# Half products for each tile of nodes in a graph layer, with the first group of rows tile by tile and the end of the last stage reordered

## The chip, the cores and the metric

The kernel runs on one core of a Trainium2 chip. A core has five engines, each with an instruction queue that it works off in order: TensorE (PE, matrix products; its weight loads are listed as PEld), VectorE (DVE), ScalarE (ACT), GpSimd (POOL) and SyncE (SP, which only issues transfers). Transfers are carried out by DMA engines and are issued by SP, ACT and POOL. The metric is the time of one execution on the device in microseconds (us). All times in the tables below are from one profiled execution, unless the text says that they are the medians of timed runs.

## The reference

The layer takes 6250 nodes with 256 features, and 100000 edges sorted by target, with 64 features each.

```python
xn = layernorm(x)
x1 = x + gnn(xn) + mix(xn)
out = x1 + ffn(layernorm(x1))

# gnn: messages along edges, summed by target
msg  = relu(xn[src] + edge_attr @ We + be)
z    = xn + segment_sum(msg, dst, N)
h    = relu(relu(z @ W1 + b1) @ W2 + b2) + xn
gnn  = layernorm(h) * gamma + beta

# mix: linear attention with 8 heads, then an MLP 256 -> 1024 -> 256
xm  = layernorm(xn) * ln1_w + ln1_b ;  xm = xm @ Wx.T + bx
q, k, v = softmax(xm Wq, features), softmax(xm Wk, nodes), xm Wv
h   = q @ (k.T @ v) @ Wo.T + bo + xn
mix = gelu(layernorm2(h) @ W1.T + b1) @ W2.T + b2 + h

# ffn: 4 experts; the gates come from a 4-head graph attention over the same edges
#   (with self loops): softmax over each node's incoming edges, layernorm, top 2 of 4
ffn = sum over experts e of  gate[:, e] * (gelu(x W1[e] + b1[e]) @ W2[e] + b2[e])
```

All of it is computed in float32.

## The kernel before

**Tiles.** Nodes lie in 49 tiles of 128 rows (the last is shorter), in 13 groups of up to four tiles. Edges lie in blocks: a block (q, 99 of them) has eight tiles of 128 edge slots and serves a window of 128 nodes. Windows advance by 64 nodes from block to block, so a tile of nodes k gets its sums from the blocks around 2k, and a block of even q serves the upper half of one node tile and the lower half of the next.

**Phase A** (to about 98 us) loads x group by group, normalises it twice (the layer's own norm, then that of the mixer), stores the rows xb that the edges will gather and the rows z that the sums are added to, and makes xm, stored as xmT. For each group DVE takes the statistics, ACT the square roots (L258), DVE the reciprocals and shifts (L262, L263), ACT the affine y (L266), DVE xn (L547), POOL xb (L550). It also reads edge indices and checks that they fit the blocks; a branch at its end (L434) takes another way for edges that don't.

**Phase B** (about 98 to 1276 us) has two strands that share the engines.

- The edge strand. POOL gathers rows of xb by the edges' sources, 128 rows in a transfer, 782 transfers (L408), into four buffers of four tiles each. TensorE multiplies the edge features by We into PSUM (msg, L1241), DVE adds the gathered rows (m, L1227, frees the gather's buffer), ACT applies the relu (L1229). For each block DVE builds two selection matrices: S, that says which slot of 32 an edge adds to (L1212), and W, that says which node of the window a slot belongs to (L1215). TensorE multiplies S with m into ps (L1259; four groups of columns, 32 wide), ACT copies ps to SBUF (left, L1263), TensorE multiplies W with left (win, L1266), DVE adds win to the rows of z (add_sums, L1188).
- The node strand. First the key-value part of the attention over all nodes, with a sort of the edges' keys (L677, L678 on DVE, L687 on TensorE); then for each group of nodes attention (attn, L1000), the mixer's MLP (L1040, L1056), and, when the sums of the group are in, the graph's MLP (L1082, L1093, z at L1104) and the norm of the result, with the head products of the graph attention (hT, L1166).

**Phase C** (about 1278 to 2407 us) runs the four experts on TensorE (L1611, L1629, outputs to DRAM as y) while POOL gathers a 32-wide row for each edge in sorted order, 784 transfers (G, L1329), in 14 chunks. DVE turns each chunk into running softmax sums by scans along the edges (attend, L1409 to L1455; the sums are stored to DRAM as sum_d, L1458). When a range of nodes has its sums, POOL gathers them (gm, L1653), share computes the gates, and weigh loads a tile's y and x1 (L1753, L1755), weighs the four experts on DVE (L1759), and stores the output (L1762). The tail after the last G gather has the last two chunks, the last gates and the last six tiles of outputs.

**What sets the order.** Each strand is a Python generator whose steps name an engine, a guessed length, what buffers they take and drop, and a rank. A planner (`Plan`) goes through all steps with the guessed lengths: it takes the step that can begin first, and among those on that engine that can begin nearly as early, the one of the lowest rank. The order that results is written out by hand as each engine's queue: the guesses decide the order, the chip decides the times. A gather of four tiles is guessed at 5.0 us and one of phase C at 1.255 us.

The number of PSUM banks for general use in phase B is four, beside two double buffers for msg.

In phase B the code around the window product, before, is:

```python
            yield step(PE, mm(1, 256), take=["bank"], drop=["left", "W"], rank=of_edges)
            pw = bank("win")
            nc.tensor.matmul(pw[:, :D], W[p0:p1, :], left[p0:p1, :], start=True, stop=True)
```

Of the kernel before, what the change touches and what calls it, by code (L numbers as in the profile page):

```python
# [17 lines left out]
P = 128  # L18
# [118 lines left out]
def gps_layer_kernel(ctx: ExitStack, tc: tile.TileContext, a: dict, out: bass.AP):  # L137
# [7 lines left out]
    NUE = a["srcT"].shape[1]  # L145
    assert NUE % 2 == 0 and NU - EG < NUE <= NU
    CG = NE // P
# [63 lines left out]

    def load_row(name, n, pool=const, col0=0):

        t = pool.tile([P, n], F32, name="r_" + name)
        src = a[name]
        nc.scalar.dma_start(t, bass.AP(tensor=src.tensor, offset=src.offset, ap=[[0, P], [1, n]]))
        return t
# [106 lines left out]

    load_x(0)
    load_x(1)
    be = load_row("be", D, ep)
    wx = load("WxT", [P, KD, D], ep)
    ln1w = load("ln1_w", [P, KD], ep)
    ln1b = load("ln1_b", [P, KD], ep)  # L330
    bx = load("bx", [P, KD], ep)
    bdq = eb.tile([P, P], F32, name="bdq")
# [159 lines left out]
    for g in range(NG + 3):  # L492
        if g < NG:
            t0, nt, cols = group(g)
            xt = xts.pop(g)
            load_x(g + XAHEAD)
            for i in range(nt):
                ln_stats(mu_var[:, t0 + i, :], xt[:, i, :], rows(t0 + i), pa)
            rs2 = pa.tile([P, GW], F32, tag="rs2", name="rs2")
            nm2 = pa.tile([P, GW], F32, tag="nm2", name="nm2")  # L500
            for r, f, n in parts(t0, nt):
                ts = slice(t0 + f, t0 + f + n)
                ln_root(rs1[:, ts], mu_var[:, ts, :], r)

                ln_root(rs2[:, f:f + n], mu_var[:, ts, :], r, scale=1.0 + EPS, add=eps2)
# [31 lines left out]
        if g < NG:  # L537
            t0, nt, cols = group(g)
            xn = pa.tile([P, GW, D], F32, tag="xn", name="xn")
            xb = pa.tile([P, GW, D], F32, tag="xb", name="xb")  # L540
            y = ys[g] = pa.tile([P, GW, D], F32, tag="y", name="y")
            for r, f, n in parts(t0, nt):
                ts = slice(t0 + f, t0 + f + n)
                ln_shift(rs1[:, ts], nm1[:, ts], mu_var[:, ts, :], r)
                ln_shift(rs2[:, f:f + n], nm2[:, f:f + n], mu_var[:, ts, :], r)
                for i in range(f, f + n):
                    nc.vector.tensor_scalar(xn[:r, i, :], xt[:r, i, :], mu_var[:r, t0 + i, 0:1],  # L547
                                            rs1[:r, t0 + i:t0 + i + 1], op0=OP.subtract, op1=OP.mult)
                    affine(y[:, i, :], xt[:, i, :], r, rs2[:, i:i + 1], nm2[:, i:i + 1])
                nc.gpsimd.tensor_tensor(xb[:r, f:f + n, :], xn[:r, f:f + n, :],  # L550
                                        be[:r].unsqueeze(1).to_broadcast([r, n, D]), OP.add)
                nc.sync.dma_start(node_rows(xb_d, t0, r, f, n), xb[:r, f:f + n, :])
                nc.sync.dma_start(node_rows(z0_d, t0, r, f, n), xn[:r, f:f + n, :])
# [21 lines left out]
    nc.vector.tensor_copy(kmr, pr[:, :KD * P].rearrange("p (k c) -> p k c", k=KD))  # L575
    by_hand.close()
    early.close()
# [3 lines left out]
    pmsg = psum.enter_context(tc.tile_pool(name="pmsg", bufs=2, space=PSUM))  # L581
    by_hand = ctx.enter_context(ExitStack())
    by_hand.enter_context(tc.manual_schedule(engines=EVERY))

# [79 lines left out]
    def sort():  # L664
# [72 lines left out]
        for w in sorted({w for _, w in chunks}, reverse=True):  # L737
            first = [o for o, w_ in chunks if w_ == w]
            o0 = first[0]
            for o in first:  # L740
                if o == first[-1] or o + w * P not in first:
# [13 lines left out]
    plan = Plan(dict(bank=4, msg=2, xm=0, x=NXH, x_=1, hm=NXH, hm_=1, r4=R4, hT=1, qT=2, xn=1, mv=6,  # L755
                     xg=XG - 0, ea=EA, S=2, W=2, m=2, left=2, z=ZB))
    plan.when.update({("xm", 0, g): 0.0 for g in first_order[:2]})
# [422 lines left out]

    def add_sums(pw, k, p0, p1):

        if not 0 <= k < NT:
            return
        p1 = min(p1, rows(k))
        if p0 < p1:
            z = zs[k // GW]
            nc.vector.tensor_add(z[p0:p1, k % GW, :], z[p0:p1, k % GW, :], pw[p0:p1, :D])  # L1188

    def sum_loads():  # L1190
# [16 lines left out]
    def block_kinds():  # L1207

        for q in range(NQ):
# [3 lines left out]
                                    slot[:, q * EG:(q + 1) * EG].unsqueeze(2).to_broadcast([P, EG, SLOT]), OP.is_equal)  # L1213
            W = ew.tile([P, P], F32, tag="W", name="W", bufs=2)
            nc.vector.tensor_scalar(W, iotaf if q % 2 else iotah, spot[:, q:q + 1], None, op0=OP.is_equal)  # L1215
# [28 lines left out]
    def sums():  # L1244

        for q in range(NQ):
            hs = halves(q)
# [8 lines left out]
            for b in range(2):  # L1256
                for i in tiles[b::2]:
                    j = i // 2
                    nc.tensor.matmul(ps[j * SLOT:(j + 1) * SLOT, :D], S[:, i, :], ms[i // 4][:, i % 4, :],  # L1259
                                     start=b == 0, stop=b == 1)  # L1260
            yield step(ACT, act(256), take=["left"], drop=["bank"], rank=0)
            left = ew.tile([P, D], F32, tag="left", name="left", bufs=2)
            nc.scalar.activation(left[p0:p1], ps[p0:p1, :D], AF.Copy)  # L1263
            yield step(PE, mm(1, 256), take=["bank"], drop=["left", "W"], rank=of_edges)
            pw = bank("win")
            nc.tensor.matmul(pw[:, :D], W[p0:p1, :], left[p0:p1, :], start=True, stop=True)  # L1266
            yield step(DVE, vec(256, 1 if q % 2 else 2), drop=["bank"], rank=1, give=[("sums", q)],
                       need=[("z", min(k // GW, NG - 1)) for k in ([q // 2] if q % 2 else [max(q // 2 - 1, 0), q // 2])])
            if q % 2:
                add_sums(pw, q // 2, 0, P)  # L1270
            else:
                add_sums(pw, q // 2 - 1, P // 2, P)
                add_sums(pw, q // 2, 0, P // 2)

# [42 lines left out]
    assert len(sure) == early[-1][2]  # L1317
    GBUFS, RING, PREP = 5, 7, 4
    SLOTS = dict(bank=6, at=2, G=GBUFS, A=2, prep=PREP, ring=RING, yo=3, hT=2, lT=2, ac=4)
    plan = Plan(SLOTS)  # L1320
# [69 lines left out]
    def attend(o, w):  # L1390

        R = 0 if w < CW else 2
        yield step(DVE, vec(4 * w, 2) + vec(0), rank=R, take=["at"], need=[("ready", o), ("G", o)])
# [12 lines left out]

        yield step(DVE, 0.35 * NH + vec(0, 2), rank=R)
        for h in range(NH):
# [5 lines left out]
        cm = yield from carried(T2, D2, NH, OP.add, OP.max, car[1], "car1", o)  # L1414
        yield step(DVE, 0.35 * NH + vec(0), rank=R)
        M = tl("M", NH, w + 1)
# [25 lines left out]
        for c0 in range(0, ROW, 5):  # L1442
            yield step(DVE, 0.3 * 5, rank=R)
            for c in range(c0, c0 + 5):
                nc.vector.tensor_tensor_scan(S[:, c, :], dk[:, head[c], :], G[:, :, c], 0.0, op0=OP.mult, op1=OP.add)
# [6 lines left out]
        for c0 in range(0, ROW, 5):  # L1452
            yield step(DVE, 0.35 * 5, rank=R, drop=["at", "prep"] * (c0 + 5 == ROW))
            for c in range(c0, c0 + 5):
# [188 lines left out]
    def share(t0, t1, need):  # L1643

        R = 4 if t1 < NT else 0
        ts, n = slice(t0, t1), t1 - t0
# [101 lines left out]
    def weigh(t, need, gates):  # L1748

        r, b = rows(t), t * P  # L1750
        yield step(SP, 0.8, rank=4, take=["ring", "ac"], need=need)
        y = ring([NX, D], F32, "y")
        nc.sync.dma_start(y[:r], y_d[t // GW, :r, :, t % GW, :])  # L1753
        ac = pc.tile([P, D], F32, tag="ac", name="ac", bufs=4)
        nc.sync.dma_start(ac[:r, :], x1_d[b:b + r, :])  # L1755
        for e in range(0, NX, 2):
            yield step(DVE, 1.0, rank=5 if t < early[-1][0] else 0, drop=["ring"] * (e == NX - 2), need=gates)
            for e_ in range(e, e + 2):
                nc.vector.scalar_tensor_tensor(ac[:r, :], y[:r, e_, :], gate[:r, t, e_:e_ + 1], ac[:r, :],  # L1759
                                               op0=OP.mult, op1=OP.add)  # L1760
        yield step(SP, 0.4, rank=4, drop=["ac"])
        nc.sync.dma_start(out[b:b + r, :], ac[:r, :])  # L1762

    def shares(some):
        for t0, t1, c in some:
            if t1 == NT:

                yield step(SP, 0, need=[("gate", early[-3][0])])
                for t in range(t0, t1):
                    spawn(weigh(t, [("y", t // GW, e) for e in range(NX)], [("gate", t0)]))  # L1770
                yield from share(t0, t1, [("sum", chunks[c - 1][0])])
                return
            yield from share(t0, t1, [("sum", chunks[c - 1][0])])
            for t in range(t0, t1):
                spawn(weigh(t, [("y", t // GW, e) for e in range(NX)], [("gate", t0)]))

    spawn = plan.spawn
    for thread in (gathers_of(sure), places(), experts(), scatter_starts(), prepare(sure), shares(early[:-1]), shares(early[-1:])):
        spawn(thread)
# [105 lines left out]
```

## Time and profile before

| what | us |
|---|---|
| timed runs, median of 3 (lowest to highest) | 2468.9 (2466.7 to 2469.7) |
| the profiled execution, its own time | 2467.7 |
| its span | 2465.9 |
| PE busy | 1997.3 |
| DVE busy | 1590.8 |
| ACT busy | 898.9 |
| POOL busy | 1703.3 |
| 782 gathers of edge rows (L408), busy | 795.1 |
| 784 gathers of phase C (L1329), busy | 768.5 |
| first gather of phase C starts | 1278.5 |
| last gather of phase C starts | 2406.4 |

A group's row in the profile gives the line, the engine, the operation, output and input by the program's names with their shapes, how many of them there were, then their busy time together and the mean of one in ns, and at the end the engine's idle time just before them and what it was that ended most of it. A row of the timeline gives the start in us, the length, the same names, how many records it stands for, and in brackets the idle time before it. A TensorE product in float32 is two records. Matrix products are pipelined, so the sum of their records may exceed the time that they take. A row of waits gives the waiting engine and operation, what it waited for, the total, the number of times and the longest. Times of the execution are shown against the span's start.

### The profile page before, as it was taken

The page shows a single profiled execution, that of the slowest core. Times are in us where ns is not written, and L with a number is a line of the kernel's source. Part 1 is how long each engine was busy: PE and PEld are TensorE (multiplying, and loading weights), DVE is VectorE, ACT ScalarE, POOL GpSimd, SP SyncE. Part 2 cuts the span into 40 slices and gives each one's busy share as a digit, 9 for nine tenths or more (in the row PEclk, how much of TensorE's full clock was granted, in tenths as well). Part 3 has the DMA queues.
Part 4 walks back from the last instruction along what each step waited for, and adds up shares of the span by engine and source line. Part 5 has one row for each costly group of instructions (what it writes and reads, how often), then busy time and mean ns, then how long its engine had stood idle before and what let it go on. Part 6 is the DMA issues. An engine that isn't in the chain of part 4 may idle for free.

```text
span 2465.9 us, 30623 instructions
## 1 busy us (share of the span) xinstructions
PE 1997.3 (81%) x10156; PEld 1297.9 (53%) x10156; DVE 1590.8 (65%) x4328; ACT 898.9 (36%) x1429; POOL 1703.3 (69%) x1701
## 2 busy tenths in 40 slices
PE   6897889998899898999969999978578898986000
PEld 3484555565565565566546776644245565655000
DVE  7588886674687786888736771119757456426566
ACT  5544645555555455665521002112222131212001
POOL 5417777777677777777327777777777777777771
PEclk9998999999999998999989999989789999998555
DMA  8865457767655545554341111212335445224522
GB/s 261 283 198 177 141 156 226 225 192 241 205 148 152 159 132 166 155 149 122 93 133 25 13 46 52 62 45 78 85 95 181 113 137 167 67 57 113 176 50 72
DMA packets 243957, 329.65 MB, mean 134 GB/s; under 512 B 49504, under 2 KB 187010, under 8 KB 242374
## 3 DMA queue, kind: packets, MB, share of 16 engines
q1 hardware_dynamic: 176678, 209.82, 26.1%
q0 software_dynamic: 65776, 116.46, 19.1%
q8 instruction: 84, 1.38, 0.2%
q10 hardware_dynamic: 1328, 1.26, 0.2%
q14 instruction: 91, 0.75, 0.1%
HBM read 227.34 MB, written 100.04 MB: 133 GB/s over the span
## 4 chain that ended last, share of the span: by engine, by line
POOL 35%; PE 25%; issue 14%; DVE 10%; DMA 9%; ACT 2%; SPq 0%; DVEq 0%; POOLq 0%; ACTq 0%
POOL G L1329 22%; POOL xg L408 9%; DMA xg<-xb_d,srcI 6%; PE hist L1491 5%; PE ffn L1040 3%; DVE m L1227 3%; PE msg L1241 3%; PE ffn L1056 3%; PE e L1629 2%; POOL st_d L1563 2%; POOL gm L1653 2%; PE e L1611 2%; PE g L1093 1%; PE ps L1259 1%; PE g L1082 1%
## 5 line engine op out<-in xcount | busy, mean ns | idle before, releaser
L408 POOL DMA_INDIRECT xg<-xb_d,srcI x782 | 795.1, 1017 | 314.3 <-issue 208.1
L1329 POOL DMA_INDIRECT G<-tab_d,srcs x784 | 768.5, 980 | 317.5 <-issue 238.6
L1589 ACT ACTIVATE hT<-e,w_eb 128x512 f32<-128x512 f32 (+1 forms) x208 | 136.3, 661 | 732.8 <-PE e L1629 712.0
L1629 PE MATMUL e<-lT,ew 128*128 128x512 f32 (+1 forms) x832 | 365.9, 587 | 17.6 <-DMA lT<-xlT_d 10.4
L1611 PE MATMUL e<-ew,hT 128*128 128x256 f32 (+1 forms) x1568 | 364.4, 389 | 4.0 <-DVE yo L1593 1.6
L1611 PEld LDWEIGHTS e<-ew,hT 128*128 128x128 f32 (+1 forms) x1568 | 302.5, 195 | 68.8 <-issue 21.1
L1227 DVE TENSOR_TENSOR m<-msg,xg 128x1024 f32<-128x1024 f32 x196 | 234.1, 1217 | 128.3 <-DMA xg<-xb_d,srcI 78.0
L1229 ACT ACTIVATE m<-m 128x1024 f32<-128x1024 f32 x196 | 205.7, 1053 | 187.9 <-DVE m L1227 184.4
L1241 PE MATMUL msg<-we,ea 64*128 64x256 f32 x1564 | 225.6, 415 | 48.7 <-DVE m L1227 43.6
L1629 PEld LDWEIGHTS e<-lT,ew 128*128 128x128 f32 x832 | 153.7, 195 | 178.8 <-issue 152.6
L1593 DVE TENSOR_TENSOR yo<-e,b 128x256 f32<-128x256 f32 (+1 forms) x196 | 79.0, 419 | 233.2 <-PE e L1611 233.1
L1241 PEld LDWEIGHTS msg<-we,ea 64*128 64x128 f32 x1564 | 143.5, 194 | 130.3 <-DVE m L1227 88.7
L1341 PE MATMUL cT<-ident,T 128*4 128x128 f32 (+1 forms) x42 | 13.4, 319 | 223.1 <-DVE T L1411 70.4
L1040 PE MATMUL ffn<-yT,w_mW1T 128*128 128x512 f32 (+1 forms) x416 | 191.3, 587 | 1.0 <-ACT hT L1030 0.5
L1056 PE MATMUL ffn<-w_mW2T,hT 128*128 128x256 f32 (+1 forms) x784 | 187.5, 387 | 0.0
L1056 PEld LDWEIGHTS ffn<-w_mW2T,hT 128*128 128x128 f32 (+1 forms) x784 | 146.0, 191 | 36.9 <-issue 15.2
L1501 DVE TENSOR_TENSOR oh<-iotar,hl 128x1024 bf16<-128x1024 bf16 (+1 forms) x256 | 123.1, 555 | 43.4 <-PE hist L1491 43.4
L1491 PE MATMUL hist<-oh 128*64 128x128 bf16 x1024 | 125.7, 418 | 9.5 <-DMA b<-in_eb 9.5
L1341 PEld LDWEIGHTS cT<-ident,T 128*4 128x4 f32 (+1 forms) x42 | 3.6, 86 | 232.1 <-issue 121.0
L1259 PE MATMUL ps<-m,S 128*32 128x256 f32 x1564 | 110.0, 397 | 15.4 <-ACT yT L1018 7.7
L1491 PEld LDWEIGHTS <-oh 128*64 128x64 bf16 x1024 | 101.6, 198 | 37.0 <-issue 12.6
L1040 PEld LDWEIGHTS ffn<-yT,w_mW1T 128*128 128x128 f32 x416 | 74.7, 195 | 73.6 <-issue 67.2
(382 smaller groups left out, 2909.9 us busy)
## 6 DMA issues: line engine op xcount, KB each, us to landing
ea<-in_eaQ SPq DMA_DIRECT2D x99, 256.0 KB
y_d<-yo SPq DMA_DIRECT2D x48, 512.0 KB
y<-y_d SPq DMA_DIRECT2D x48, 512.0 KB
sum_d<-zf SPq DMA_DIRECT2D x32, 512.0 KB
G<-tab_d,srcs POOLq DMA_INDIRECT x784
xg<-xb_d,srcI POOLq DMA_INDIRECT x782
xm<-xmT_d SPq DMA_DIRECT2D x23, 512.0 KB
sum_d<-G SPq DMA_DIRECT2D x11, 1024.0 KB
```

Of the source, the lines that this page charges most:

```text
L408: nc.gpsimd.indirect_dma_start(out=xg, out_offset=None, in_=xb_d[:, :], in_offset=bass.IndirectOffsetOnAxis(ap=srcI[:, u:u + 1], axis=0))
L1040: nc.tensor.matmul(ps[:, :cols], mw1[:, k, c * P:(c + 1) * P], yTs[g][:, k, :cols], start=k == 0, stop=k == KD - 1)
L1056: nc.tensor.matmul(ps[:r, :D], hT[0][:, c, i * P:i * P + r], mw2[:, c, :], start=c == 0, stop=c == MC - 1)
L1227: nc.vector.tensor_add(m[:, :n, :], ps[:, :n, :], xgs.pop(q * EG + 4 * s)[:, :n, :])
L1229: nc.scalar.activation(m[:, :n, :], m[:, :n, :], AF.Relu)
L1241: nc.tensor.matmul(ps[:, i % 4, :], lh, rh, start=True, stop=True)
L1259: nc.tensor.matmul(ps[j * SLOT:(j + 1) * SLOT, :D], S[:, i, :], ms[i // 4][:, i % 4, :], start=b == 0, stop=b == 1)
L1329: nc.gpsimd.indirect_dma_start(out=rows_of[o][:, c, :], out_offset=None, in_=tab_d[:, :], in_offset=bass.IndirectOffsetOnAxis(ap=srcs[:, o ...
L1491: nc.tensor.matmul(hist[0][b * KHI:(b + 1) * KHI, :P], hi[:, :, b * HG // 2 + i], lo[:, :, b * HG // 2 + i], start=c0 + i == 0, stop=c0 + ...
L1589: nc.scalar.activation(hT[:, c, :cols], ps[:, :cols], AF.Gelu, bias=b1[:, e * XC + c:e * XC + c + 1])
L1611: nc.tensor.matmul(ps[:r, :D], hT[:, c, i * P:i * P + r], w2s[e][:, c, :], start=c == 0, stop=c == XC - 1)
L1629: nc.tensor.matmul(ps[:, :cols], w1s[e][:, k, c * P:(c + 1) * P], lTs[g][:, k, :cols], start=k == 0, stop=k == KD - 1)
```

## The change

- Group 0 of x is loaded as four transfers, one for each tile, and all work of phase A on it that took the group at once (roots, shifts, affine, xn, xb, the stores) goes by tiles. The loads of be, WxT, ln1_w, ln1_b and bx are issued by SP, not by ACT.
- The hand-written order is no longer closed and opened again between phase A and phase B.
- In phase B the window product of a block (128 columns) becomes half products: for each tile of nodes, once the three blocks that touch it have their `left`, four products of 64 columns each accumulate into one PSUM bank, and DVE adds the bank to the tile's rows of z once. W has five buffers for two, left four for two; a `left` that isn't filled over all 128 rows is cleared first.
- In phase C there are eight buffers for ac, not four; the last chunk's `attend` goes ahead of the others in rank; the scans' guessed lengths depend on the chunk's width; `share` and `weigh` have other ranks; the loads for the last two ranges of nodes (tiles 43 to 48) are made known to the planner once the gates of tiles 39 to 42 are done, and those tiles' outputs are stored by ACT, not by SP.

```diff
-    load_x(0)
+    def pieces(g, t0, nt):
+        return [(P, i, 1) for i in range(nt)] if g == 0 else parts(t0, nt)
+    xts[0] = pa.tile([P, GW, D], F32, tag="xt", name="xt", bufs=XAHEAD + 2)
+    for r, f, n in pieces(0, 0, GW):
+        nc.sync.dma_start(xts[0][:r, f:f + n, :], node_rows(a["x"], 0, r, f, n))
     load_x(1)
-    be = load_row("be", D, ep)
-    wx = load("WxT", [P, KD, D], ep)
+    be = load_row("be", D, ep, nc.sync)
+    wx = load("WxT", [P, KD, D], ep, nc.sync)
...
-            for i in range(nt):
-                ln_stats(mu_var[:, t0 + i, :], xt[:, i, :], rows(t0 + i), pa)
-            for r, f, n in parts(t0, nt):
+            for r, f, n in pieces(g, t0, nt):
                 ts = slice(t0 + f, t0 + f + n)
+                for i in range(f, f + n):
+                    ln_stats(mu_var[:, t0 + i, :], xt[:, i, :], r, pa)
...
-    by_hand.close()
     early.close()
     psum.close()
...
-    by_hand = ctx.enter_context(ExitStack())
-    by_hand.enter_context(tc.manual_schedule(engines=EVERY))
...
-                     xg=XG - 0, ea=EA, S=2, W=2, m=2, left=2, z=ZB))
+                     xg=XG - 0, ea=EA, S=2, W=5, m=2, left=4, z=ZB))
...
+        lefts = {}
+
+        def by_node(k):
+            yield step(PE, 1.1, take=["bank"], drop=["left", "W"] * 2, rank=1)
+            pw = bank("win")
+            for b in range(2):
+                for h in range(2):
+                    W, left = lefts[2 * k + b + h]
+                    s = slice(h * WIN, (h + 1) * WIN)
+                    nc.tensor.matmul(pw[s, :D], W[:, s], left, start=b == 0, stop=b == 1)
+            yield step(DVE, vec(256), drop=["bank"], rank=1, need=[("z", k // GW)], give=[("sums", 2 * k + 2)])
+            r = rows(k)
+            z = zs[k // GW][:r, k % GW, :]
+            nc.vector.tensor_add(z, z, pw[:r, :D])
...
+            left = ew.tile([P, D], F32, tag="left", name="left", bufs=4)
+            if p1 - p0 < P:
+                nc.vector.memset(left, 0.0)
             nc.scalar.activation(left[p0:p1], ps[p0:p1, :D], AF.Copy)
-            yield step(PE, mm(1, 256), take=["bank"], drop=["left", "W"], rank=of_edges)
-            pw = bank("win")
-            nc.tensor.matmul(pw[:, :D], W[p0:p1, :], left[p0:p1, :], start=True, stop=True)
-            yield step(DVE, vec(256, 1 if q % 2 else 2), drop=["bank"], rank=1, give=[("sums", q)], ...
-            if q % 2:
-                add_sums(pw, q // 2, 0, P)
-            else:
-                add_sums(pw, q // 2 - 1, P // 2, P)
-                add_sums(pw, q // 2, 0, P // 2)
+            lefts[q] = W, left
+            if q and q % 2 == 0:
+                spawn(by_node(q // 2 - 1))
...
-        R = 0 if w < CW else 2
+        R = -1 if (o, w) == sure[-1] else 0 if w < CW else 2
-        yield step(DVE, 0.35 * NH + vec(0, 2), rank=R)
+        yield step(DVE, (0.09 + 0.004 * w) * NH + vec(0, 2), rank=R)
...
-        R = 4 if t1 < NT else 0
+        R = -1 if t1 == NT else 1 if t1 == early[-2][1] else 4
...
-        yield step(SP, 0.8, rank=4, take=["ring", "ac"], need=need)
+        at_end = t >= early[-2][0]
+        yield step(SP, 0.8, rank=4 if at_end else 3, take=["ring", "ac"], need=need)
...
-            yield step(DVE, 1.0, rank=5 if t < early[-1][0] else 0, drop=["ring"] * (e == NX - 2), need=gates)
+            yield step(DVE, 1.0, rank=3 if t < early[-1][0] else 0, drop=["ring"] * (e == NX - 2), need=gates)
...
-        nc.sync.dma_start(out[b:b + r, :], ac[:r, :])
+        (nc.scalar if at_end else nc.sync).dma_start(out[b:b + r, :], ac[:r, :])
...
-    for thread in (gathers_of(sure), ..., shares(early[:-1]), shares(early[-1:])):
+    for thread in (gathers_of(sure), ..., shares(early[:-2]), shares(early[-2:-1]), shares(early[-1:])):
```

## The prediction

> **What bounds the kernel now.** I read the page's totals first, then the busy time of each engine by stage, then the list of waits, then the timeline of the bounding queue at the seams. No engine is full over the whole span. The two stretches below (span, then sum and count for PE, weight load, DVE, ACT and POOL, then clock and DMA share) show two stages with different limits.
>
> ```profile
> PE 1997.3 (81%) x10156; PEld 1297.9 (53%) x10156; DVE 1590.8 (65%) x4328; ACT 898.9 (36%) x1429; POOL 1703.3 (69%) x1701
> 100.00:1276.00 1176.00, 1061.27 (x6358) 688.71 (x6358) 866.35 (x1708) 631.45 (x988) 793.88 (x781) 0.96 0.56 167
> 1276.00:2407.00 1131.00, 857.67 (x3552) 570.12 (x3552) 609.30 (x2148) 197.05 (x300) 857.45 (x876) 0.87 0.33 90
> ```
>
> From 100 to 1276 us (phase B) TensorE is busy 1061 of 1176 us, and POOL's gathers, 0.95 to 1.02 us each with 0.30 us of issue, run almost as full. From 1276 to 2407 (phase C) POOL does nothing but issue: 876 transfers in 1131 us are 1.29 us each, their own pace, so that stage is POOL's.
>
> ```profile
> POOL xg L408 <- DVE m L1227: 26.2, 21, 6.4
> PE msg L1241 <- DVE m L1227: 43.6, 28, 4.2
> DVE m L1227 <- DMA xg<-xb_d,srcI: 78.0, 34, 6.6
> DVE z L1188 <- PE win L1266: 36.7, 24, 2.9
> ```
>
> These waits between 190 and 1276 us (total, times, longest) tell that inside phase B the edge stream (gather, message product, add m) is late in both directions: POOL waits for m to free a buffer, and m waits far more often for the gather to land. TensorE waits for m too. So TensorE's lead over the gathers, and what it still has to do when the last gather is in, set the end of phase B. The timeline of the seam, and of the tail:
>
> ```profile
> 622.08 0.95 POOL L408 DMA_INDIRECT xg<-xb_d,srcI  x1 [6.44 <-DVE m L1227]
> ...
> 1200.27 1.10 POOL L408 DMA_INDIRECT xg<-xb_d,srcI  x1 [0.30 <-issue]
> 1204.43 1.13 PE L1241 MATMUL msg<-we,ea 64*128 64x256 f32 x4
> 1254.58 13.98 PE L1056 MATMUL ffn<-w_mW2T,hT 128*128 128x256 f32 x64
> 1278.48 0.95 POOL L1329 DMA_INDIRECT G<-tab_d,srcs  x1 [77.12 <-DVE iotar L1472]
> 2406.39 0.94 POOL L1329 DMA_INDIRECT G<-tab_d,srcs  x1 [0.30 <-issue]
> 2410.48 3.61 DVE L1455 TENSOR_TENSOR_SCAN G<-both,cr,G 128x32 f32<-128x32 f32 x20
> 2456.96 2.05 DVE L1759 SCALAR_TENSOR_TENSOR ac<-y,gate,ac 128x256 f32<-128x256 f32 x4 [1.11 <-DMA ac<-x_d]
> ```
>
> The last edge gather starts at 1200.27, the last message product at 1204.43, ending at 1205.5; TensorE then works off 70 us of node work, with hardly a gap, until 1275.7, while POOL idles 77 us. Phase C begins at 1278.5. So a microsecond won in B or A before that point moves the end one for one, and so does work put behind the last message.
>
> **The change, step by step.** The sum is made against the profiled execution, 2467.7 us (span 2465.9 and 1.8 around it), which lies 1.2 below the median 2468.9.
>
> Head. Group 0 of x now comes in four one-tile loads, its norms, affines and stores go tile by tile, and five weight loads leave ACT's queue for SP's. Added: twelve small shifts on DVE, six roots on ACT, three loads, six stores. On SP the later x groups queue behind the five loads and a wait for an earlier slot, about 9.5 to 13 us instead of early, but DVE has its first tile at 5.83 and reaches groups 2 and 3 after 20.
>
> ```profile
> 11.37 1.28 ACT L258 ACT_TABLE_LOAD   x1 [11.37 <-DMA r_be<-in_be]
> 13.69 2.08 ACT L266 ACTIVATE y<-xt,nm,rs 128x256 f32<-128x256 f32 x4 [0.54 <-DVE nm L263]
> ```
>
> ACT issues loads until 11.34, although the statistics of group 0 are done at 8.05. Freed of five issues it can load its table at about 6.2, finish the first root near 9.3 and begin y there: 4 us sooner, 3.3 for DVE's xn (ends 14.95 now). After that DVE has almost no idle time up to 72 us, so a gain of DVE carries through phase A. Since the queues are no longer closed between A and B, DVE also no longer builds two blocks' S and W in phase A (0.9 to 1.4 us), but POOL issues its first gathers after the branch at 104.39 instead of two before it (up to 2 us lost; POOL's wait there is 3.18). I take -4.5; ends -6.5 (all of it, DVE's 0.9 too) and -2 (the branch takes the gathers' 2 us and the late x loads cost DVE its 1.06 us wait for the z store again).
>
> Sums. Per block one window product and 1 or 2 adds go; per node tile come four products 64 columns wide and one add.
>
> ```profile
> L1188 DVE TENSOR_TENSOR z<-z,win 64x256 f32<-64x256 f32 x96 | 40.2, 419 | 15.0 <-PE win L1266 13.0
> L1259 PE MATMUL ps<-m,S 128*32 128x256 f32 x1564 | 110.0, 397 | 15.4 <-ACT yT L1018 7.7 <-ACT hT L1030 4.0 <-DVE z L1188 2.5
> L1266 PE MATMUL win<-left,W 128*128 128x256 f32 x194 | 66.3, 424 | 5.8 <-ACT left L1263 2.1 <-DVE z L1104 1.3 <-DVE adst_all L1172 1.0
> ```
>
> DVE: 98 adds fewer at 0.41, 40 us of 866, and most of the 36.7 us in which it stood in order behind a window product. Neither is the bound of B; it is worth what it takes from the stalls below. TensorE: products on separate column groups run beside each other in the ps row (16 records of 0.397 us take 1.0 us of the timeline, four groups at a time). Four half-width products in two groups, two records each, then take about 1.0 us, the two old ones 0.52 each: nothing on balance. Ends: 49 x 1.0 more if the halves run one after another (+49), and 49 x -0.5 if they pair fully (-24). I take 0, since the ps row has the same form.
>
> The trace has a price for switching between forms: a visit to ps takes 1.00 us where its records at four groups alone make 0.93. The Trainium skill, TensorEngine Tiling (Array Packing), Key Properties, has a rule that speaks against this change: changing the tiling mode drains TensorE. The window product is 128*128 like its neighbours now and would be 128*64, so by that rule with the 0.07 of the row, 49 visits would add an estimated 3.4 us and the sum would be 2485.3 in place of 2481.9, which leaves it out.
>
> Stream of the gathers. POOL's big stalls after the key-value part (373, 449, 535 and 622 us, 20.1 us together) have one cause: DVE stands in order behind a graph MLP and its norm while the next m is due.
>
> ```profile
> 612.63 0.69 DVE L1104 TENSOR_TENSOR z<-g,r_gb 128x512 f32<-128x512 f32 x1 [7.84 <-PE g L1093]
> 620.58 2.36 DVE L1227 TENSOR_TENSOR m<-msg,xg 128x1024 f32<-128x1024 f32 x2
> ```
>
> In the built order of the changed kernel the node work between those two instructions grows, not shrinks: at four of these places the norm and its neighbours ahead of the next m make 11.9 for 9.7, 11.9 for 9.7, 11.9 for 11.5 and 17.7 for 15.0 us by their rows. That is 7.5 us more in stalls if nothing else moves; the 36.7 us of waits for window products that go give part of it back. I take +4 on the stream, ends +8 and -12 (half of the 26.2 us of waits for m gone). The last gather starts at 1200.27 - 4.5 + 4 = 1199.8.
>
> Order on TensorE. This is the term that decides. By the built order TensorE has, ahead of the same message, as much other work as before up to message 630 and then 7 to 23 us less; what is left moves behind the last message: 24 more L1056 products (0.478 us each, 11.5), 8 more L1040 (0.97 each, 7.8), 8 attn (3.8), 8 qT (1.2), 16 turns (2.3), 8 g products (0.8), one hT (0.3), and 0.5 less of win: +27.2, on 70.2 now. TensorE reaches the last message sooner, but can't start it before the gathers are in: the gather six earlier starts at 1191.6, lands 3.5 later, its m takes 1.2 and the hand-over 0.3, so the last message ends about 1198.3 (6 to 7 us better than 1205.5, where TensorE itself was late). Phase B ends at 1198.3 + 97.4 = 1295.7, against 1275.7: +20. Ends: +15 and +25 (a fifth of the moved work, either way, that fits gaps or is met by new ones).
>
> Phase C. Eight ac buffers, new ranks and guessed lengths change the order on DVE, SP and ACT; POOL's 784 gathers, 49 scatters and 43 gm stay, at 1.29 each, with 1.5 us of waits in all: 0, ends +4 and -4 (the gm groups move by a few gathers).
>
> Tail. After the last gather lands (2408.83) DVE scans the second-last chunk for 3.61 us; 15 of these 20 scans now come before, about 2.7. Its gm gathers follow sooner, and loads of the last two node groups are issued before the last sum stores, so the 1.11 wait goes. ACT's six output stores stand behind nothing late: its next table load has 1.2 us to spare. With about 2 for the reordered sums, -5.8; ends -2.7 and -9.
>
> Sum: 2467.7 + 20 (in which head and stream are counted) + 0 - 5.8 = 2481.9.
>
> **A second rule.** After a 3.15 us wait TensorE's next products ran slow:
>
> ```profile
> 602.07 1.13 PE L1241 MATMUL msg<-we,ea 64*128 64x256 f32 x8 [3.15 <-DVE m L1227]
> 603.13 3.41 PE L1056 MATMUL ffn<-w_mW2T,hT 128*128 128x256 f32 x8
> ```
>
> Eight such records otherwise take 1.9, so a wait costs 1.5 us beyond itself. The Trainium skill, TensorE: Matmul & The Clock Gate, HAM oscillation, warns of idle gaps on TensorE above some 3.4 us, after which its clock falls; a TensorE that runs ahead and waits for gathers would have more of them, and each would add about an estimated 1.5 us by that row. The granted clock of 0.96 in B doesn't separate this; nothing in the sum uses it.
>
> **The rivals.** *The stalls go, and the order pays (faster).* DVE is freed of 40 us and 36.7 us of waits, the gathers run nearer their quiet 1.25 us, and TensorE stays the bound all through B: then B ends at 1275.7 - 4.5, the tail gives 5.8, 2457.4. For it: the 26.2 us of POOL's waits for m, and 1061 busy of 1176. Against it: the 78.0 us in which m waits for a gather, and the longer blocks ahead of m. It decides if the last gather starts before 1180 (27.2 us sooner on TensorE's last message); the sign turns at about 1186, 14 us before my 1199.8.
>
> *The halves run one after another (slower still).* +49 on a TensorE that bounds B: 2481.9 + 49 = 2531. For it only the 128*64 form, which before has only with bf16 in hist; against it the four groups of ps side by side.
>
> *Nothing that can be told.* TensorE's surplus behind the last message is half hidden and the stream gains a few us: about +10 at the end of B, less 5.8 and some: within 4.9 us (0.2%, what a measurement here can tell from none) of 2468.9.
>
> **How the numbers follow.** Likeliest 0.64, faster rival 0.23, serial halves 0.04, nothing 0.09. Its own range goes from 2470 (+15 in B, stream 6 better, tail -9 with +4 in C) to 2493 (+25, +4 in C, tail -2.7). The whole range reaches down to the faster rival, 2452, with its head at -6.5 and its tail at -9, and leaves the serial halves out. Faster 0.25, same 0.11, slower 0.64, from these cases and their edges.
>
> **What would show it.** Right: last edge gather near 1200, TensorE's node work after the last message near 97 us, the first G gather near 1298, phase C still 1128 us long, from there to the end some 6 us less after the last G gather, y beginning at about 9.5. Wrong: the stalls at 373 to 622 gone, and the last gather before 1186; window rows taking 2 us a tile; or an output store late on ACT.

## The result, and the profile after

The changed kernel takes 2473.9 us (median of 17 runs, 2468.1 to 2478.9), the kernel before 2467.6 (17 runs beside them). The ratio is 1.0029, with a 95% interval of 1.0018 to 1.0040: slower by 4 to 10 us. The forecast was 14 us slower, 2481.9.

The profiled execution has a span of 2470.9 us, 5.0 more than before. The seams of its timeline say where they arise. First POOL's timeline at the two seams (start, length, operation, idle time before it in brackets), then TensorE's last message and last product of phase B:

```profile
1184.37 0.95 POOL L414 DMA_INDIRECT xg<-xb_d,srcI  x1 [0.30 <-issue]
1293.79 0.95 POOL L1334 DMA_INDIRECT G<-tab_d,srcs  x1 [108.47 <-DVE iotar L1477]
2419.30 0.94 POOL L1334 DMA_INDIRECT G<-tab_d,srcs  x1 [0.30 <-issue]
2427.67 0.94 POOL L1658 DMA_INDIRECT gm<-sum_d,end_i  x1 [7.43 <-DVE both L1431]
```

```profile
1181.50 1.13 PE L1235 MATMUL msg<-we,ea 64*128 64x256 f32 x4
1290.76 0.37 PE L1169 MATMUL hT<-ident,heads__30200 64*128 64x64 f32 x1 [0.43 <-ACT heads__30200 L1166]
```

| | before | after | difference |
|---|---|---|---|
| last edge gather starts | 1200.3 | 1184.4 | -15.9 |
| last message starts on TensorE | 1204.4 | 1181.5 | -22.9 |
| last product of phase B starts | 1275.3 | 1290.8 | +15.5 |
| first G gather to last G gather | 1127.9 | 1125.5 | -2.4 |
| last G gather to the end of the span | 59.5 | 51.6 | -7.9 |

So the tail is better and phase B worse. In phase B the edge strand is ready 16 to 23 us sooner, and nevertheless TensorE, which has the same work but for the half products, finishes 15 us later. What stands behind the last message takes it 109 us where it took 71. The busy time in phase B (PE, weight load, DVE, ACT, POOL, then clock, DMA share and GB/s), the waits for m and of m between 190 and 1291 us (total, times, longest), and the rows of the edge gathers and of the half products:

```profile
101.00:1291.00 1190.00, 1069.10 (x6552) 678.53 (x6552) 829.95 (x1614) 637.32 (x993) 782.97 (x781) 0.95 0.55 165
```

```profile
PE msg L1235 <- DVE m L1221: 53.6, 37, 5.2
POOL xg L414 <- DVE m L1221: 22.6, 17, 4.9
DVE m L1221 <- DMA xg<-xb_d,srcI: 104.5, 55, 7.7
```

```profile
L414 POOL DMA_INDIRECT xg<-xb_d,srcI x782 | 784.6, 1003 | 309.1 <-issue 210.9
L1250 PE MATMUL win<-left,W 128*64 128x256 f32 x392 | 54.1, 398 | 0.1
```

DVE is busy for 36 us less, as the change meant. Against 1061 us busy of 1175 before (101 to 1276), TensorE is busy for 1069 of 1190: 8 us more of busy time, and 7 us more of idle time, of which the wait for a message's PSUM to come free (msg behind m) makes 10. m in turn waits 104.5 us for gathers that haven't landed, 78.0 before: the messages are asked for earlier than the gathers deliver them.

### The profile page after: what moved, and what is told of

It is laid out like the page before. It is cut to its first block, busy times and chain, and to the rows that moved or that the text cites. A ratio compares the mean times of both kernels' runs of the same rounds, so it can differ in the third digit from the quotient of the medians.

```text
span 2470.9 us, 30876 instructions
## 1 busy us (share of the span) xinstructions
PE 2016.3 (82%) x10350; PEld 1292.5 (52%) x10350; DVE 1559.0 (63%) x4244; ACT 912.6 (37%) x1445; POOL 1692.2 (68%) x1704
## 5 line engine op out<-in xcount | busy, mean ns | idle before, releaser
L414 POOL DMA_INDIRECT xg<-xb_d,srcI x782 | 784.6, 1003 | 309.1 <-issue 210.9
L1616 PE MATMUL e<-ew,hT 128*128 128x256 f32 (+1 forms) x1568 | 373.3, 394 | 4.8 <-ACT hT L1594 4.0
L1221 DVE TENSOR_TENSOR m<-msg,xg 128x1024 f32<-128x1024 f32 x196 | 236.7, 1219 | 167.9 <-DMA xg<-xb_d,srcI 104.5
L1235 PE MATMUL msg<-we,ea 64*128 64x256 f32 x1564 | 224.8, 411 | 54.6 <-DVE m L1221 53.6
L1043 PE MATMUL ffn<-yT,w_mW1T 128*128 128x512 f32 (+1 forms) x416 | 195.0, 600 | 2.7 <-ACT hT L1033 2.2
L1043 PEld LDWEIGHTS ffn<-yT,w_mW1T 128*128 128x128 f32 x416 | 73.5, 196 | 84.6 <-issue 73.8
```

The lines of the kernel that those rows point to most:

```text
L414: nc.gpsimd.indirect_dma_start(out=xg, out_offset=None, in_=xb_d[:, :], in_offset=bass.IndirectOffsetOnAxis(ap=srcI[:, u:u + 1], axis=0))
L1043: nc.tensor.matmul(ps[:, :cols], mw1[:, k, c * P:(c + 1) * P], yTs[g][:, k, :cols], start=k == 0, stop=k == KD - 1)
L1221: nc.vector.tensor_add(m[:, :n, :], ps[:, :n, :], xgs.pop(q * EG + 4 * s)[:, :n, :])
L1235: nc.tensor.matmul(ps[:, i % 4, :], lh, rh, start=True, stop=True)
L1616: nc.tensor.matmul(ps[:r, :D], hT[:, c, i * P:i * P + r], w2s[e][:, c, :], start=c == 0, stop=c == XC - 1)
```

## Experiments: which part costs what

Two theories were set against each other. *Order*: the half products are neutral in themselves, but their steps move the order that the planner writes for TensorE, and this is a worse order. *Price*: the half products themselves cost TensorE time, through changes of form, whatever the order.

**The head alone** (the first group by tiles, five loads on SP, no seam between A and B; the kernel before elsewhere).

```diff
+    for r, f, n in pieces(0, 0, GW):
+        nc.sync.dma_start(xts[0][:r, f:f + n, :], node_rows(a["x"], 0, r, f, n))
...
+    wx = load("WxT", [P, KD, D], ep, nc.sync)
...
-    by_hand.close()
```

> The kernel before with the head alone: first group by tiles, five weight loads on SP, no seam in the hand-written order between phases A and B. Both theories: in the changed kernel phase A ended only 0.3 us sooner and the first edge gathers 2.5 us sooner, so 1 to 3 us faster, about 2465.5. If the head were worth the 4.5 us that was forecast, 2463.

Measured: 2470.2 against 2470.0 for the kernel before on the same chip, ratio 1.000 (0.9988 to 1.0013). No gain that can be told, where 1 to 3 us, or the forecast's 4.5, had been expected. The rows of the changed kernel's DVE timeline below (first shift, one of the slow ones, last xn of group 0) show where the 4 us went: the shifts begin at 9.22 in place of 13.00, but by tiles they and xn last until 14.41, 5.2 us in place of 1.95 (13.00 to 14.95), with twelve more shifts, three of which took 0.7 us in place of 0.16. Each of these three began just after one of POOL's additions for xb (L556, 0.72 us each) and ended 0.02 us after it or less. The group was done 0.5 us sooner, no more.

```profile
9.22 0.17 DVE L262 RECIPROCAL rs<-rs 128x1 f32<-128x1 f32 x1 [0.80 <-ACT rs L258]
...
10.28 0.71 DVE L263 SCALAR_TENSOR_TENSOR nm<-mu_var,rs 128x1 f32<-128x1 f32 x1
...
14.00 0.41 DVE L553 TENSOR_SCALAR xn<-xt,mu_var,rs 128x256 f32<-128x256 f32 x1
```

**The half products alone.**

```diff
-            pw = bank("win")
-            nc.tensor.matmul(pw[:, :D], W[p0:p1, :], left[p0:p1, :], start=True, stop=True)
...
+                    nc.tensor.matmul(pw[s, :D], W[:, s], left, start=b == 0, stop=b == 1)
```

> The kernel before with the half products alone. Theory 'order' (the new steps move the planner's order on TensorE, so that about 100 us of node products stand behind the last message where 70 did) and rival 'price' (the half products themselves cost TensorE time, by changes of form) both expect the whole loss here: 2467.6 plus 14 to 17, 2482 to 2485, last edge gather 12 to 16 us sooner than 1200, TensorE done 14 to 17 us later than 1276. If the loss came from the parts together, 2470 or less.

Measured: 2487.9, ratio 1.0075 (1.0055 to 1.0095), 14 to 23 us slower. Last edge gather at 1185.95, last product of phase B at 1293.15. The loss is all here, as both theories had it, 3 us above their 2482 to 2485.

**Phase C alone.**

```diff
+    SLOTS = dict(..., ac=ACS)
...
+        R = -1 if (o, w) == sure[-1] else 0 if w < CW else 2
...
+        (nc.scalar if at_end else nc.sync).dma_start(out[b:b + r, :], ac[:r, :])
```

> The kernel before with the changes of phase C alone. Both theories: 8 us less behind the last G gather and 2 less in phase C, as in the changed kernel: 2456 to 2459. If the 2 us of phase C came from the late start there, 2460.

Measured: 2459.4, ratio 0.9956 (0.9942 to 0.9970), 10.6 us faster (7 to 14). From the last G gather to the end 51.7 us, as in the changed kernel. This run also tells how far single profiles can be trusted: its phase B is that of the kernel before, and yet its last edge gather started at 1206.53 and its first G gather at 1287.26, 6.3 and 8.8 us later than there. What stood behind the last message took 71 us in both. The three parts add up: 0 + 17.9 - 10.6 = +7.3, where the changed kernel lost 6.3.

**The same instructions in another order.** The planner's guess for four edge gathers goes from 5.0 to 5.4 us; in the kernel before, the 749 gathers that start from 190 us on came every 1.35 us, waits included, 5.4 for four. Without waits they take 0.95 and 0.30 of issue, 5.0 for four.

```diff
-            yield step(POOL, 5.0, take=["xg"], give=[("xg", u)])
+            yield step(POOL, 5.4, take=["xg"], give=[("xg", u)])
```

> The changed kernel, with the planner told that four edge gathers take 5.4 us, not 5.0: the built order then has about 47 us of node products behind the last message in place of 93, and the same instructions. Theory 'order': phase B ends 12 to 25 us sooner than in the changed kernel, near 1270, the whole 2450 to 2462. Rival 'price': the order matters little, since TensorE's products themselves take longer: phase B still ends after 1285, the whole 2468 or more.

Measured: 2417.0, ratio 0.9785 (0.9764 to 0.9805): 53 us faster than the kernel before, 57 faster than the changed kernel. That is beyond what theory *order* had expected (2450 to 2462), and out of reach for *price*: these are the half products, all of them. POOL's seam, TensorE's busy time in phase B, and its longest wait:

```profile
1169.10 1.02 POOL L414 DMA_INDIRECT xg<-xb_d,srcI  x1 [0.30 <-issue]
1231.70 0.95 POOL L1334 DMA_INDIRECT G<-tab_d,srcs  x1 [61.58 <-DVE di L1481]
```

```profile
101.00:1227.00 1126.00, 1049.94 (x6552) 665.45 (x6552) 831.34 (x1614) 646.17 (x1000) 784.97 (x781) 0.98 0.57 174
```

```profile
PE msg L1235 <- DVE m L1221: 29.1, 24, 4.0
```

What stands behind the last message now takes TensorE 60 us (1167.06 to 1226.72) in place of 109, and the last message itself comes 14 us sooner. Three more things are to be seen. TensorE's wait for messages falls from 53.6 to 29.1 us; its idle time in phase B from 121 to 76; and its busy time, for the same 6552 products, from 1069 to 1050 us at a granted clock of 0.98 for 0.95. The gathers end 15 us sooner as well, although the planner was told that they are slower. Both strands gain from this order.

**Does the kernel before gain from the same guess?** The kernel before, with the guess changed and nothing else (its runs on other chips stand further down):

```diff
-            yield step(POOL, 5.0, take=["xg"], give=[("xg", u)])
+            yield step(POOL, 5.4, take=["xg"], give=[("xg", u)])
```

> The kernel before with 5.4 us guessed for four edge gathers; two tries gave 0.987 and 0.989 of the kernel before, on a chip where that took 3681 us. Theory 'order': 25 to 45 us faster where the kernel before takes 2470, 2425 to 2445. The changed kernel at 5.4 took 2417, 2428 without the 10.6 of phase C: a result above 2428 is the half products' gain in a mended order. Rival, 'only the half products need the other guess': 2465 to 2475.

Measured: 2424.8, ratio 0.9827 (0.9803 to 0.9850), 43 us faster than the kernel before. TensorE in phase B:

```profile
101.00:1239.00 1138.00, 1051.13 (x6358) 679.67 (x6358) 866.88 (x1708) 644.58 (x998) 801.81 (x782) 0.98 0.58 172
```

```profile
PE msg L1241 <- DVE m L1227: 29.3, 21, 5.8
```

Its last message started at 1194.73 and its last product of phase B at 1238.21: 43 us behind the last message in place of 71.

So the poor order isn't a fault of the half products alone: the kernel before had lost 43 us to the same guess of 5.0, and the changed one 57. With the guess mended, the change as a whole is worth 0.9785 - 0.9827 = -0.0042, with an error of 0.003 by the two intervals: 10 us, faster, about what phase C gave by itself (10.6). For the half products and the head nothing is left that can be told, 0 within some 9 us. Theory *order* stands; of *price* nothing shows: in the mended order TensorE is busy for 1050 us with half products and 1051 without.

**The freed DVE.** Two spare adds for each tile of nodes, of the same operands, into the unused half of the bank; the order elsewhere as in the changed kernel.

```diff
+            for _ in range(2):
+                nc.vector.tensor_add(pw[:r, D:], z, pw[:r, :D])
             nc.vector.tensor_add(z, z, pw[:r, :D])
```

> The changed kernel with 98 spare adds, the order elsewhere unchanged. If the freed 40 us of DVE brought the 16 us by which the last edge gather came sooner, it goes back to about 1200; if the order on TensorE brought it, it stays within 5 us of 1184. The whole 2474 to 2480 in both.

Measured: 2480.5, ratio 1.0055 (1.0037 to 1.0073), at the upper end of what was expected; the intervals of this and of the changed kernel just touch. The last edge gather is at 1191.13, 6.8 us later than in the changed kernel and between the two expectations. Two profiles of one and the same phase B lay 6.3 us apart, so this doesn't decide between them. Its gathers, behind those of the kernel before:

```profile
L408 POOL DMA_INDIRECT xg<-xb_d,srcI x782 | 795.1, 1017 | 314.3 <-issue 208.1 <-DVE m L1227 74.3 <-DMA xg<-xb_d,srcI 8.8
L414 POOL DMA_INDIRECT xg<-xb_d,srcI x782 | 792.6, 1014 | 308.4 <-issue 208.8 <-DVE m L1221 69.2 <-DMA xg<-xb_d,srcI 10.5
```

The gathers themselves are longer than in the changed kernel, 792.6 us for 784.6. Over the profiles on chips where the kernel before takes 2468 to 2470 us, the count of adds and the length of the gathers go together: with 147 window adds on DVE the 782 gathers take 795, 798, 798 and 803 us (the kernel before, the head alone, phase C alone, the kernel before at 5.4), with 49 adds 785, 786 and 787 (the changed kernel, half products alone, the changed kernel at 5.4), with 49 and 98 spare ones 793. That looks like about 0.1 us of gather for an add, but the timeline says otherwise. The first two rows are of the kernel before, the last two of the run with spare adds:

```profile
518.42 1.22 DVE L981 TENSOR_TENSOR q<-q,qsm 128x1024 f32<-128x1024 f32 x1
518.54 1.93 POOL L408 DMA_INDIRECT xg<-xb_d,srcI  x1 [0.30 <-issue]
...
318.28 0.88 DVE L1255 TENSOR_TENSOR win<-z,win 128x256 f32<-128x256 f32 x2
318.45 0.95 POOL L414 DMA_INDIRECT xg<-xb_d,srcI  x1 [0.30 <-issue]
```

A gather that ran beside window adds took its usual 0.95 us; one that ran beside a step of the attention with two operands in SBUF (q, qsm) took 1.93 and ended 0.83 us behind it. Sorted over the whole of phase B, the gathers beside a step of the sort on DVE (key; its minima and maxima read two operands in SBUF as well) took 35.9 us more than 0.944 us each in the kernel before (198 gathers), 27.3 in the changed one (196) and 33.5 with spare adds (194); those beside window adds and no other DVE instruction but m took 0.1 us more in all, in each of the three (26, 18 and 47 gathers). So the adds don't lengthen the gathers; what they run beside does, and that differs from order to order; how the spare adds came to change it, no run shows. Of the 15.9 us by which the last gather came sooner, 10.5 are shorter gathers; most of the rest, 5.2, is idle time of POOL (314.3 before, 309.1 after), less waiting for m above all.

**On two chips where the kernel before takes 3681 and 3685 us.** Six runs, of four kernels, fell on such chips: the kernel before at 5.4 and the spare adds, once on each, and on the first the changed kernel at 5.6, and the changed kernel with the edges' rank for its half products on TensorE, as the window products had it:

```diff
-            yield step(PE, 1.1, take=["bank"], drop=["left", "W"] * 2, rank=1)
+            yield step(PE, 1.1, take=["bank"], drop=["left", "W"] * 2, rank=of_edges)
```

> The kernel before, with the planner told 5.4 us for four edge gathers in place of 5.0; built order: 39 us of node products behind the last message in place of 67. Theory 'order': this helps the kernel before too, by 25 to 45 us, 2425 to 2445. Set beside the run with half products and 5.4, less the 10.6 that the changes of phase C gave alone, it prices the half products with the order mended: at 2428 they are worth nothing, above it they gain. A rival, 'the half products need the other guess': the kernel before doesn't gain, 2465 to 2475.

> The changed kernel with 5.6 us for four edge gathers: by the built order 10 us of node products behind the last message, 22 us more of them ahead of the messages in the last third. Theory 'order' with TensorE as the bound: nothing more to gain, last message later by what is moved ahead of it, 2412 to 2430. If what is left behind the last message were itself the loss, another 30 us: 2385 to 2395.

> The changed kernel with the half products' rank on TensorE put back to that of the window products before (the edges' rank, 0 or 6, in place of 1), gathers guessed at 5.0: built order 10 us behind the last message. If it is the rank 1 of the new step that spoiled the order, the loss of the half products goes with it: 2457 or less; by theory 'order' even 2410 to 2435. Rival 'price': 2470 or more.

> The changed kernel with two more adds of the same operands for each tile of nodes, into the unused half of the product's bank (98 in all, about 40 us of DVE, as many as the half products took away), the same order elsewhere. The last edge gather of the changed kernel stands 16 us sooner than before. If the freed DVE brought that, it goes back to about 1200 and TensorE's end moves little or not, 2474 to 2480; if the order on TensorE brought it, the gather stays within 5 us of 1184.

> Again the kernel before with 5.4 us guessed for four edge gathers, since the chip of the first try took 3681 us for the kernel before. Theory 'order': 25 to 45 us faster, 2425 to 2445. With the 10.6 us of phase C added to the changed kernel at 5.4 (2417, so 2428 without them), a result above 2428 is what the half products gain once the order is mended, one at 2428 says that they gain nothing. Rival, 'only the half products need the other guess': 2465 to 2475.

> Again the changed kernel with 98 spare adds (40 us of DVE) where its half products are added, the order elsewhere unchanged, for the same reason. If the freed DVE brought the 16 us by which the last edge gather came sooner, it goes back to about 1200; if the order on TensorE did, it stays within 5 us of 1184. The whole 2474 to 2480 in both.

Measured there, as ratios to the kernel before on the same chip: the kernel before at 5.4, 0.987 (0.982 to 0.991) and 0.989 (0.985 to 0.992); the changed kernel at 5.6, 0.974 (0.970 to 0.978); the changed kernel with the edges' rank, 1.0045 (1.0021 to 1.0069); spare adds, 1.002 (0.999 to 1.005) and 1.001 (0.998 to 1.003). None of the expectations in us can be held to these. The direction of the guess is the same there; putting back the rank didn't repair the order there; whether it would on the other chips, and whether 5.6 is better than 5.4, stays open. The run with the edges' rank shows that little work behind the last message doesn't make a good order by itself: 28 us are left there, for 107 to 108 with the spare adds, but its last edge gather started at 1609.8, 83 to 103 us later than with them, and phase B ended no sooner. The spare adds don't show in the gathers there: 775 and 780 us, for 774 and 778 without them (edges' rank, 5.6).

What makes these chips slow isn't settled. In the profile of the spare adds on the second of them DVE and ACT are busy as long as on the faster chip (1601 us for 1598, 915 for 914; m 1217 ns, as in the kernel before), TensorE longer (2265 us for 2014, at a granted clock of 0.78 for 0.91). There are waits that nothing in the profile ends, on TensorE, DVE and ACT, and phase C takes 1967 us from its first to its last G gather in place of 1124. Two of those waits, of products and of copies in the expert networks; the waits of the kernel before on the faster chip have no such row for either group:

```profile
PE e L1618 <- issue: 341.3, 72, 19.5
DVE yo L1600 <- issue: 228.9, 13, 57.7
```

## Why the prediction was right, and where it wasn't

The sign and the place were right: TensorE's work behind the last message decides, phase B ends later, and the tail gives a part back. The sum was 14.2 us and 6.3 were measured (5.0 between the two profiled executions), and that it came out within the range is in part luck, because terms of both signs were off.

- *Head, -4.5.* It gave 0 (-3 to +3). The step that failed is the count of what was added: twelve shifts on DVE were named and not priced. They and the tile-wise xn took 3.2 us of the 3.8 by which ACT's root came sooner; the first y began at 10.39, not at about 9.5.
- *Sums on TensorE, 0.* Right. The eight records of a tile's half products take 1.01 us of the timeline (1180.49 to 1181.50, and the median of all 49), the window products before 0.54 each, two for a tile. The rival of serial halves (+49) is out: by it they would take 2 us. The Trainium skill, TensorEngine Tiling (Array Packing), Key Properties, has TensorE drain when the form changes, which the prediction had estimated at 3.4 us and left out. The runs show no sign of it: in the mended order TensorE is busy for 1050 us with the half products and 1051 without, though 3.4 us would hardly stand out. The 0.93 us behind that estimate stands in no row: the records of a visit to ps start four by four, 0.22 us apart, which makes 0.86 of its 1.00.
- *Stream of the gathers, +4.* It was -15.9, beyond its lower end of -12. What failed, on the DVE time that the change frees: "Neither is the bound of B; it is worth what it takes from the stalls below". The stalls were to grow by 7.5 us; the five longest waits of POOL after the key-value part (358 to 698 us) make 18.0 us, where the four before made 20.1, and its waits for m went from 26.2 to 22.6. The larger part, 10.5 us, came from shorter gathers, a term that I had not seen in the row of 1017 ns: I took the gathers as 0.95 to 1.02 us each, whatever DVE does beside them.
- *Order, +20 at the end of phase B.* +15.5 in the profile, by another split: the last message ended at 1182.6, not 1198.3, and the work behind it took 108.5 us, not 97.4. What moved behind the last message was nearly what the forecast had counted (24 more L1056 products, 8 more L1040, 8 attn); I had counted it from the built order at best rates, and TensorE without waits. The rows of the timeline behind the last message show what was missing: with the edge strand gone nothing fills TensorE's waits for ACT and DVE, and the first products after a wait run slowly.

```profile
1189.14 1.08 PE L993 MATMUL qT<-ident,q 128*128 128x128 f32 x4 [2.32 <-DVE q L984]
1190.01 3.04 PE L1085 MATMUL g<-zT,w_gW 128*128 128x256 f32 x8
1218.40 1.24 PE L938 MATMUL tr<-ident,y 128*128 128x128 f32 x8 [2.51 <-ACT hT L1033]
1219.56 3.68 PE L1043 MATMUL ffn<-yT,w_mW1T 128*128 128x512 f32 x4
1226.41 0.55 PE L938 MATMUL tr<-ident,z 106*128 106x106 f32 x2 [2.60 <-DVE z L1254]
1226.97 3.33 PE L1043 MATMUL ffn<-yT,w_mW1T 128*128 128x512 f32 x4
```

  Four records of L1043 took 1.9 us elsewhere; after waits of 2.51 and 2.60 us they took 3.68 and 3.33, at a granted clock of 0.54 and 0.55 (1219.5 to 1223.2, 1227.0 to 1230.2; 1.00 between, from 1223.2 to 1226.3). The Trainium skill, TensorE: Matmul & The Clock Gate, HAM oscillation, speaks of gaps above some 3.4 us; here waits of 2.3 us were enough (0.61 from 1190.0 to 1193.0), and the measurement decides. Behind the last message TensorE was idle for 12 of 109 us at a mean clock of 0.94, before for 4.5 of 70 at 0.98.
- *The faster rival's condition, "the sign turns at about 1186".* It fell: the last gather started at 1184.4 and the kernel was slower; of the two signs that I had named together for being wrong, the early gather came and the stalls stayed. The condition took the work behind the last message as done sooner whenever the message is; but it is the order's own, and an early message that TensorE waits for, or that leaves node work behind, wins nothing.
- *Phase C and tail, 0 and -5.8.* -10.6 when run alone (-7 to -14), -2.4 and -7.9 in the profile. From the last G gather to the first gm gather 8.4 in place of 11.1, the 2.7 as forecast; to the second range's gm gathers 13.2 for 15.3; the last weighing has no wait for a load; and the stores that ACT issues end 1.8 us sooner behind it, which I had put at nothing. The tail is firm: 51.6 to 51.7 us in the four profiles with these changes on the faster chips, 57.8 to 60.0 in the four without. The 2.4 in phase C need no cause: from the first to the last G gather the profiles without these changes range from 1123.3 to 1129.7.

## What to carry to other kernels

Where a planner with guessed lengths writes the queues, vary its guesses before judging an edit: the order from a guess of 5.0 us for four gathers, their time without waits, cost the kernel before 43 us and the changed one 57 against the order from 5.4, their pace with waits. That is several times all that the edit itself could bring. That 5.4 is best because it is the measured pace isn't shown: with 5.6 the changed kernel ran on another chip only, and took 0.974 of the kernel before there. An edit that is neutral by its own instructions can still lose by the order that it brings; the same instructions in another order are the experiment that tells. The version to keep is the changed kernel with 5.4, 2417 us, 0.9785 of the kernel before.

## What was not expected of the hardware

POOL's gathers take longer beside some instructions of DVE: 1.93 us in place of 0.95 beside q, 35.9 us longer in all beside the sort's steps in the kernel before, but 0.95 beside window adds. The Trainium skill, SBUF — State Buffer, SBUF: two separate sides, has DVE and GpSimd block each other where DVE reads two operands from SBUF and the GpSimd operation reads SBUF too; q and the sort do read two from SBUF, the window adds read one of theirs from PSUM, and the rows agree with that.

TensorE's rate falls after waits as short as 2.3 us: eight records of g took 3.04 us, where the same eight took 1.99 before. The wait alone doesn't tell, though: after one of 2.53 us that ended at 1162.43 the clock stayed at 1.00. The three falls shown above each lasted 3.4 us, and in the 3.4 us ahead of each TensorE was busy for 1.3, 1.2 and 0.8 us; but 3.4 us with 0.9 us of work, from 1159.0 to 1162.4, brought no fall. What decides stays open.

And two chips took 49% longer for the same kernel, with waits without a releaser; their cause isn't settled.
